# A mixture-of-experts kernel: 102 of 105 expert blocks in the main loop, the last three behind a branch at the end

## The chip, the core and the metric

The kernel runs on one core of a Trainium2 chip. A core has five engines with instruction queues of their own: TensorE (PE, matrix products; its weight loads are listed as PEld), VectorE (DVE), ScalarE (ACT), GpSimd (POOL) and SyncE (SP, which here only issues transfers), and 16 DMA engines that move data between DRAM and the on-chip memory. The engines run side by side and wait for each other by semaphores. The metric is the device time of one execution in microseconds (us).

## What is computed

The input `x` has the shape (2, 256, 56, 56): two images of N = 3136 positions and C = 256 channels. The first layer is a linear attention without softmax, with batch norm, residual and ReLU. The second layer treats the positions as tokens: layer norm, causal softmax attention with four heads, residual, and then a mixture of eight experts of which each token takes two. Only the last part matters here:

```python
probs = jax.nn.softmax(xf @ gate_w + gate_b, axis=-1)
top2_vals, top2_idx = jax.lax.top_k(probs, 2)
cw = jnp.zeros((N, Ee)).at[jnp.arange(N)[:, None], top2_idx].add(top2_vals)
# for each expert, added up with weight cw:
h = jax.nn.gelu(xf @ w1 + bb1, approximate=False)   # 256 -> 512
y = h @ w2 + bb2                                    # 512 -> 256
```

Here `xf` are all 6272 tokens of both images after a second layer norm. The result is added to the tokens before that norm and laid out as (2, 256, 56, 56) again. All arithmetic is in 32-bit floats.

## The kernel before, in words

A token and one of its two experts are a *pair*; there are 2 x 6272 = 12544 pairs, 98 blocks of 128. The experts' work is done block by block: 128 pairs of one expert at a time, so each expert rounds its pairs up to whole blocks. How many blocks are used depends on the data; it is at most `NBLK = (2*B*N + E*(P-1)) // P = 105`. The kernel of before always works on all 105; blocks that hold no pair are computed on rows of zeros and their results are dropped.

The order of the blocks serves the two images. Blocks 0 to 41 (`FULL0` = 42) hold pairs of image 0 alone; blocks 42 to 56 (`MIXED` = 57) hold the rest of image 0's full blocks, eight mixed ones and, where there is room, pairs of image 1; the remaining ones hold pairs of image 1, ordered by the token chunk at which they begin. That order is worked out on the chip, in `last_blocks` (L1180 and on): `upto` holds for each expert the running number of its last block, `eblks` the expert of each block, `qblk` its place in the table `x_slots`, `b1bs` its first bias. Blocks without pairs come last.

`experts` (L1296 to 1473) runs over the blocks with everything written out by hand, in an order that the kernel fixes (`manual_schedule`). In round `n` it fetches a group of `GB` = 3 blocks of rows six blocks ahead (`fetch`, on SP), prepares their target rows (`load`, three small DVE instructions), does the first product and the gelu of block `n` (`hidden`: 8 matrix products into `ht` in two passes each, L1398, and four gelus on ACT, L1407), transposes the rows of block `n + 2` (`inputs`, `tp`, L1375), copies the first weights of a later block next to the products (`weights`, 0.7 us on DVE, L1386), and does the second product of block `n - 3` (`outputs`, `LATE` = 3: `yp`, L1417). `outputs` adds the second bias on DVE into `ys` (L1427) and writes it out. Blocks below 57 go to `y_slots` by SP, blocks from 42 on go to `y_tokens` by an indirect transfer on POOL (a scatter, L1434), one row per pair; a row that holds no pair gets an address out of bounds and is not written. `worked[0]` counts the blocks whose outputs have been issued.

At the end of each round `between()` pulls two or three steps of side work from a queue of generators. The side work in this stage is `finish(0)` and `finish(1)`, which build the output of the two images in pieces of two token chunks (12 pieces of 256 tokens, numbered 0, 2, ... 22 by their first chunk, and piece 24 of 64). For image 1 a piece is loaded from `y_tokens` (two transfers on SP, L1516, one for each of the two experts' results), added to the residual `t` with the gate's weights (`add`, DVE, L1529), transposed (`store`, TensorE into `yo`, L1541), copied (ACT, L1546) and stored (SP, L1547). A piece may be loaded when all blocks that can hold its tokens are done: `complete(n)` is the number of blocks that this takes, 57 + 2n for a piece that ends before chunk n, and at most 105. `GAP` = 2 rounds are waited beyond that, and again between load and add. When the blocks are through (`over`), the rest of the pieces is drained as fast as it goes. A load waits on SP for the scatters of the blocks that it needs, and SP works in order.

At the very end each engine reads the small integer `good` and compares it with 128: a number that `judge` (L1588) computed from the softmax sums. If the sums were out of range, a second, general version of the layer runs; on these inputs it doesn't, and each engine jumps over it.

Of the kernel before, what the change touches and what calls it, by code (L numbers as in the profile page):

```python
# [9 lines left out]
F32 = mybir.dt.float32  # L10
U32 = mybir.dt.uint32
I32 = mybir.dt.int32
AF = mybir.ActivationFunctionType
ALU = mybir.AluOpType
AX = mybir.AxisListType
PSUM = bass.MemoryType.PSUM
# [3 lines left out]
SP = mybir.EngineType.SP  # L20
# [7 lines left out]
def conv_attn_moe_kernel(  # L28
# [47 lines left out]

    nc = tc.nc
    P = 128  # L80
    B, C, N = x.shape
    NH = C // P
# [4 lines left out]
    E = gate_w.shape[1]  # L87
    H = w1.shape[2]
    KH = H // P
    NCH = -(-N // P)  # L90
# [7 lines left out]
    XS = C + 2  # L98

    OFF = 16 * N  # L100
    FULL0 = -(-(2 * N - E * (P - 1)) // P)
    MOST0 = 2 * N // P
    MIXED = MOST0 + E
    NBLK = (2 * B * N + E * (P - 1)) // P
    GB = 3
    SCALE = 1.0 / HS**0.5
    LEAST, MOST = 1e-25, 1e25
    assert B == 2 and NBLK % GB == 0 and FULL0 % GB == 0 and QB % (2 * P) == 0
# [5 lines left out]
    def pairs(first=0, end=NCH):  # L114

        n = first
        while n < end:
            m = 2 if n + 1 < end and chunk(n + 1) == P else 1
            yield n, m, chunk(n)
            n += m  # L120

    const = ctx.enter_context(tc.tile_pool(name="const", bufs=1))
    tok = ctx.enter_context(tc.tile_pool(name="tok", bufs=1))

    ident = const.tile([P, P], F32, name="ident")
# [9 lines left out]
    def rows(name):  # L135
        t = room(name)[:, : NCH * XW].rearrange("p (n w) -> p n w", w=XW)
        if chunk(NCH - 1) < P:
            nc.gpsimd.memset(t[chunk(NCH - 1) :, NCH - 1, :], 0.0)
        return t
# [15 lines left out]
    def stats(b, n, m, k, pool, nm):  # L155

        for a in range(m):
            st6 = pool.tile([P, 6], F32, tag="st6", name=f"st6_{nm}_{n}_{a}")
            nc.vector.bn_stats(st6[:k], ts[b][:k, n + a, :C])
            nc.vector.bn_aggr(ts[b][:k, n + a, MEAN : MEAN + 2], st6[:k])  # L160

    def inverse_deviation(b, n, m):
        r = ts[b][:, n : n + m, RSTD]

        d = ts[b][:, n : n + m, SLOT]
        nc.scalar.activation(d, r, AF.Sqrt, bias=eps5)
        nc.vector.reciprocal(r, d)
# [258 lines left out]
    early = const.tile([P, MIXED], F32, name="early")  # L426
    wts = [const.tile([P, NCH, 2], F32, name=f"wt{b}") for b in range(B)]
    sums = const.tile([P, NSUM, 2 * W // P], F32, name="sums")
    good = const.tile([1, 1], I32, name="good")

    def empty_slots(b):
        nc.sync.dma_start(
# [6 lines left out]
    def layer1(nm, general):  # L439

        with ExitStack() as whole:
# [7 lines left out]
            def bank(name, shape=(P, 512)):  # L449
                return pm.tile(list(shape), F32, tag="m", name=f"{name}_{nm}")  # L450
# [484 lines left out]
            def dispatch(b):  # L935
# [244 lines left out]
                def last_blocks():  # L1180
# [5 lines left out]
                    def col(name, w=1):  # L1186
                        return g1.tile([R, w], F32, tag=name, name=f"{name}_{nm}")
# [3 lines left out]
                    edge = few("edge")  # L1191
                    nc.vector.tensor_scalar(edge[:, :1], nfull, float(E), None, ALU.add)
                    nc.vector.tensor_tensor(upto, upto, edge[:, :1].to_broadcast([P, E]), ALU.add)
                    past = col("c_past", E)
                    nc.vector.tensor_tensor(past, upto[:R], num.to_broadcast([R, E]), ALU.is_le)
                    hot = col("c_hot", E)
# [99 lines left out]
            def experts(w1s, w2s, b2s, ex, es, ps6, between, need, written):  # L1296
# [153 lines left out]
                        written()  # L1450

                fetched, groups, ids, xin, wb, act = [], [], [], {}, {}, {}
                for n in range(-1, NBLK + LATE):
                    while len(fetched) * GB <= min(n + 6, NBLK - 1):
                        fetched.append(fetch(len(fetched)))
                    while len(groups) * GB <= min(n + 3, NBLK - 1):
                        groups.append(load(len(groups), *fetched[len(groups)]))
                    if n < 0:
                        ids.extend(experts_of(0))
                    if 0 <= n < NBLK:  # L1460
                        act[n] = hidden(n, xin.pop(n), wb.pop(n))
                    for m in (n + 1, n + 2):
                        if m < NBLK and m > n + 1 - (n < 0):
                            xin[m] = inputs(m, groups[m // GB])
                    for m in (n + 1, n + 2):
                        if m < NBLK and m not in wb:
                            wb[m] = weights(m)
                    if 0 <= n - LATE < NBLK:
                        outputs(n - LATE, act.pop(n - LATE))

                    if len(ids) <= min(n + 3, NBLK - 1):
                        ids.extend(experts_of(len(ids) // GB))
                    between()

            def finish(b, oy, bufs):
# [27 lines left out]
                def complete(n):  # L1503


                    return min(NBLK, (2 * N + 2 * n * P) // P + E)

                def load(n, m, k):

# [14 lines left out]
                    return n, m, k, ys, t[:k, n : n + m, :C]  # L1524

                def add(n, m, k, ys, rows):
                    for a in range(m):
                        for c, y in enumerate(ys):
                            nc.vector.scalar_tensor_tensor(  # L1529
                                rows[:, a], y[:k, a], wts[b][:k, n + a, c : c + 1],  # L1530
                                rows[:, a], ALU.mult, ALU.add,
                            )
                        yield True

                def store(n, m, k, ys, rows):
                    w = (m - 1) * P + k
                    ot = oy.tile([P, NH, 2 * P], F32, tag="ot", bufs=2, name=f"ot_{nm}{b}_{n}")
                    yo = bank(f"yo_{b}_{n}", (P, NH, 2 * P))
                    for o in range(NH):
                        for a in range(m):  # L1540
                            nc.tensor.transpose(  # L1541
                                yo[:, o, a * P : a * P + k],
                                rows[:, a, o * P : (o + 1) * P],
                                ident[:k, :k],
                            )
                    nc.scalar.copy(ot[:, :, :w], yo[:, :, :w])  # L1546
                    nc.sync.dma_start(  # L1547
                        out=out[b, :, n * P : n * P + w].rearrange("(c p) n -> p c n", p=P),
                        in_=ot[:, :, :w],
                    )  # L1550
# [17 lines left out]
                GAP = 2  # L1568
                while parts or ahead or added:
                    now = worked[0]  # L1570
                    over = now == NBLK
                    if parts and len(ahead) < bufs:
                        n, m, k = parts[0]
                        if over or now >= complete(n + m) + GAP:
                            ahead.append((now, load(*parts.popleft())))
                            yield True
                            continue
                    if added and (over or now > added[0]):
                        store(*added[1])
                        added = None  # L1580
                        yield True
                    elif ahead and not added and (over or now >= ahead[0][0] + GAP):
                        yield from add(*ahead[0][1])
                        added = now, ahead.popleft()[1]
                    else:
                        yield False

            def judge():  # L1588

                tiles = g1.tile([P, 4], F32, tag="judge", name=f"judge_{nm}")  # L1590
                flat_sums = sums.rearrange("p r f -> p (r f)")
                nc.vector.tensor_reduce(tiles[:, 0:1], flat_sums, AX.X, ALU.max)
                nc.vector.tensor_reduce(tiles[:, 1:2], flat_sums, AX.X, ALU.min)
                yield True
                nc.vector.tensor_scalar(tiles[:, 2:3], tiles[:, 0:1], MOST, None, ALU.is_le)
                nc.vector.tensor_scalar(tiles[:, 3:4], tiles[:, 1:2], LEAST, None, ALU.is_ge)
                nc.vector.tensor_tensor(tiles[:, 2:3], tiles[:, 2:3], tiles[:, 3:4], ALU.mult)
                yield True
                yield True
                gdp = bank("gdp")  # L1600
                nc.tensor.matmul(gdp[:1, :1], tiles[:, 2:3], ones[:, 0:1], start=True, stop=True)
                nc.vector.tensor_copy(good, gdp[:1, :1])


            queue = deque()
# [167 lines left out]
            with ExitStack() as moe:  # L1773
# [40 lines left out]
                while queue:  # L1814
                    pull()

    layer1("f", False)

    n_good = nc.values_load(
        good, min_val=0, max_val=P,  # L1820
        skip_runtime_bounds_check_because="a count of at most P rows",
    )
    with tc.If(n_good < P):
        ts[0] = rows("t0g")
        for b in range(B):
            nc.sync.dma_start(out=ts[b][:, :, :C], in_=kept[b])
            with tc.tile_pool(name=f"r{b}", bufs=2) as rs:
                for n, m, k in pairs():
                    stats(b, n, m, k, rs, f"r{b}")
            inverse_deviation(b, 0, NCH)  # L1830
        layer1("g", True)


# [50 lines left out]
```

## Time and profile before

| | |
|---|---|
| time, median of 10 runs | 1319.36 us (1317.81 to 1321.12) |
| the profiled execution | 1318.74 us |
| its span, first to last instruction | 1317.0 us |
| mean TensorE clock granted | 0.993 |
| TensorE busy, 0 to 150 us (first layer) | 140.3 us |
| TensorE busy, 150 to 860 us (attention) | 700.9 us |
| TensorE busy, 860 to 1299.5 us (experts, with what is left of the attention) | 433.5 us |
| TensorE busy, 1299.5 to 1317 us (drain and end) | 2.3 us |
| `ht` matrix passes (L1398) | 1680, first at 881.9, last at 1290.7 us |
| scatters to `y_tokens` (L1434) | 63, last at 1299.3 us |
| loads from `y_tokens` (L1516) | 26, last at 1303.8 us |

A product in 32-bit floats shows as two or more passes, so a block has 16 passes of `ht`. In lists of instructions "x16" is the number of them, a name such as `ht_f<-xT_f,w_f` is the tile written and the tiles read, and "L1398" the line. In the chain of work that ended last, each row is a start, a length and the work, and each piece of work was what the next one waited for.

### The profile page before, as it was taken

To read this page: it belongs to the slowest core of one execution; us is meant where nothing else is said; L and a number is where in the kernel's file an instruction comes from. 1 tells how busy PE (TensorE), PEld (TensorE's weight loads), DVE (VectorE), ACT (ScalarE), POOL (GpSimd) and SP (SyncE) were. 2 spreads that over 40 slices of the span, in tenths; PEclk is the share of its full clock that TensorE was granted. 3 is DMA by queue.
4 is the path that set the end of the run, shared out by engine and by line. 5 is a ranking of instruction groups with operands and counts; after the bars stand their busy time and mean duration, and the time that the engine had idled before them with its cause. 6 is when DMAs were issued, how large, how long until landed. Compare 5 with 4: busy or idle time off the path is not lost.

```text
span 1317.0 us, 28242 instructions
## 1 busy us (share of the span) xinstructions
PE 1277.1 (97%) x10647; PEld 813.6 (62%) x10647; DVE 793.2 (60%) x1693; ACT 606.9 (46%) x1241; POOL 311.8 (24%) x300
## 2 busy tenths in 40 slices
PE   8999999999999999999999999999999999999995
PEld 7875444444444444444344444448999999999994
DVE  1582556657777754666868787864765443556552
ACT  0145554555555555455554456562433333344441
POOL 1113110100000111110003572000067112765541
PEclk9999999999999999999999999999999999999997
DMA  9993000000000000100001225241245333666552
GB/s 305 384 327 128 16 24 25 24 16 25 9 17 10 19 6 9 34 16 15 9 9 40 69 83 167 76 141 41 73 149 170 114 113 97 187 212 193 187 154 72
DMA packets 111048, 123.96 MB, mean 94 GB/s; under 512 B 20095, under 2 KB 100620, under 8 KB 110904
## 3 DMA queue, kind: packets, MB, share of 16 engines
q1 hardware_dynamic: 96664, 92.89, 22.6%
q0 software_dynamic: 10416, 26.00, 5.9%
q10 hardware_dynamic: 3824, 3.18, 0.8%
q8 instruction: 88, 1.44, 0.5%
q14 instruction: 56, 0.46, 0.1%
HBM read 63.04 MB, written 60.81 MB: 94 GB/s over the span
## 4 chain that ended last, share of the span: by engine, by line
PE 90%; DVE 3%; DMA 2%; ACT 1%; issue 1%; POOL 0%; SPq 0%; DVEq 0%; POOLq 0%; ACTq 0%
PE yp_f L689 20%; PE sc_f L649 19%; PE ht_f L1398 14%; PE yp_f L1417 13%; PE qk_f L535 7%; PE v_f L554 4%; PE pp_f L598 4%; PE cp L321 3%; PE gram L252 3%; PE tp_f L1375 2%; DVE acc_f L671 1%; PE sp_f L716 1%; ACT st_f L657 1%; PE yo_f L1541 1%; PE xp_f L514 1%
## 5 line engine op out<-in xcount | busy, mean ns | idle before, releaser
L657 ACT ACTIVATE st_f<-sc_f 128x896 f32<-128x896 f32 (+5 forms) x400 | 333.7, 837 | 294.4 <-PE sc_f L649 265.4
L671 DVE TENSOR_TENSOR acc_f<-acc_f,st_f 128x896 f32<-128x896 f32 (+5 forms) x372 | 366.4, 985 | 161.0 <-ACT st_f L657 153.4
L689 PE MATMUL yp_f<-st_f,v_f 64*64 64x448 f32 (+6 forms) x3184 | 340.4, 503 | 10.0 <-DVE qT_f L700 8.2
L649 PE MATMUL sc_f<-qT_f,kT_f 64*64 64x448 f32 (+6 forms) x3184 | 341.3, 500 | 0.0
L1407 ACT ACTIVATE g_f<-ht_f,b1b 128x128 f32<-128x128 f32 x420 | 119.8, 368 | 224.9 <-PE ht_f L1398 224.8
L689 PEld LDWEIGHTS yp_f<-st_f,v_f 64*64 64x64 f32 x3184 | 112.2, 133 | 162.9 <-issue 131.6
L649 PEld LDWEIGHTS sc_f<-qT_f,kT_f 64*64 64x64 f32 x3184 | 117.0, 133 | 151.3 <-issue 137.0
L1398 PE MATMUL ht_f<-xT_f,w_f 128*128 128x128 f32 x1680 | 206.6, 276 | 2.7 <-DVE w_f L1386 2.7
L1398 PEld LDWEIGHTS ht_f<-xT_f,w_f 128*128 128x128 f32 x1680 | 202.9, 193 | 7.9 <-issue 3.3
L497 POOL TENSOR_SCALAR xn_f<-t 128x256 f32<-128x256 f32 (+1 forms) x50 | 68.2, 1371 | 541.7 <-issue 331.1
L1279 POOL DMA_INDIRECT x_slots<-xr_f,idx x100 | 113.4, 1134 | 203.6 <-DVE xr_f L1271 111.6
L1386 DVE COPY w_f<-w1s_f 128x1024 f32 x105 | 73.3, 699 | 60.5 <-PE ht_f L1398 60.2
L1434 POOL DMA_INDIRECT y_tokens<-ys_f,to_f x63 | 64.5, 1024 | 135.8 <-DVE ys_f L1427 109.2
L1427 DVE TENSOR_TENSOR ys_f<-yp_f,kT_f 128x128 f32<-128x128 f32 x105 | 30.5, 291 | 105.9 <-PE yp_f L1417 105.2
L535 PE MATMUL qk_f<-px_f,wat 128*128 128x512 f32 (+1 forms) x224 | 92.6, 558 | 1.2 <-ACT px_f L520 1.2
L659 DVE TENSOR_TENSOR st_f<-st_f,keep 128x256 f32<-128x256 f32 (+1 forms) x112 | 44.1, 394 | 68.2 <-ACT st_f L657 67.8
L535 PEld LDWEIGHTS qk_f<-px_f,wat 128*128 128x128 f32 x224 | 38.7, 190 | 54.3 <-issue 44.6
L1417 PE MATMUL yp_f<-px_f,g_f 128*128 x210 | 63.0, 382 | 0.0
L1417 PE MATMUL yp_f<-kT_f,g_f 128*128 x210 | 62.5, 379 | 0.0
L1417 PE MATMUL yp_f<-w2s_f,g_f 128*128 x210 | 62.5, 379 | 0.0
L1417 PE MATMUL yp_f<-v_f,g_f 128*128 x210 | 62.5, 379 | 0.0
L1491 POOL DMA_INDIRECT y_f<-y_slots,idx x50 | 55.9, 1118 | 16.3 <-issue 13.7
(256 smaller groups left out, 1172.0 us busy)
## 6 DMA issues: line engine op xcount, KB each, us to landing
x_slots<-fill SPq DMA_DIRECT2D x1, 8127.0 KB
xb_f<-x_slots SPq DMA_DIRECT2D x63, 129.0 KB
x_slots<-fill SPq DMA_DIRECT2D x1, 7296.0 KB
y_slots<-ys_f SPq DMA_DIRECT2D x57, 128.0 KB
kept<-t SPq DMA_DIRECT2D x2, 3200.0 KB
x<-in_x_dram SPq DMA_DIRECT2D x14, 448.0 KB
xr<-in_x_rows_dram SPq DMA_DIRECT2D x12, 512.0 KB
out_dram<-ot_f SPq DMA_DIRECT2D x24, 256.0 KB
```

What stands on the lines that cost most here:

```text
L497: nc.gpsimd.tensor_scalar(xn[:k, a], ts[b][:k, n + a, :C], ts[b][:k, n + a, MEAN : MEAN + 1], ts[b][:k, n + a, RSTD : RSTD + 1], ALU.subtr ...
L535: nc.tensor.matmul(ps[:, :w], wat[:, c, d0 : d0 + P], xT[:, c, :w], start=(c == 0), stop=(c == NH - 1),)
L649: nc.tensor.matmul(ps[h : h + HS, a, c0:W], kT[hp][rows, j * P + h : j * P + h + HS], qT[rows, hp, q0 + c0 : q0 + W], start=True, stop=True,)
L657: nc.scalar.activation(st[:k, :, c0:], ps[:k, :, c0:W], AF.Exp, scale=SCALE)
L671: nc.vector.tensor_tensor(acc[:k, :, c0:], acc[:k, :, c0:], st[:k, :, c0:], ALU.add)
L689: nc.tensor.matmul(yp[a * HS : (a + 1) * HS, h // HS, c0:W], v[hp][h : h + HS, j, a, :HS], st[h : h + HS, a, c0:], start=first, stop=bool( ...
L1279: s = nc.gpsimd.indirect_dma_start(out=xds[b], out_offset=bass.IndirectOffsetOnAxis(ap=idxs[b][:kk, k, n : n + 1], axis=0), in_=xr[:kk], i ...
L1386: nc.vector.tensor_copy(w, w1s[:, :, bass.ds(e, 1), :].rearrange("p c e h -> p c (e h)"))
L1398: nc.tensor.matmul(ht[:, k, :], w[:, c, k * P : (k + 1) * P], xT[:, c, :], start=(c == 0), stop=(c == NH - 1),)
L1407: nc.scalar.activation(g[:, k, :], ht[:, k, :], AF.Gelu, bias=b1bs[b][:, k, i : i + 1])
L1417: nc.tensor.matmul(yp[:, :C], g[:, k, :], w2s[k][:, bass.ds(e, 1), :].rearrange("p e d -> p (e d)"), start=(k == 0), stop=(k == KH - 1),)
L1434: s = nc.gpsimd.indirect_dma_start(out=y_tokens, out_offset=bass.IndirectOffsetOnAxis(ap=to[:, n % GB : n % GB + 1], axis=0), in_=ys, in_o ...
```

## The change

The main loop runs over `MAIN = NBLK - GB` = 102 blocks. A flag `fits` says whether the blocks used are at most 102; it is multiplied into a second integer next to `good`. At the end the engines read the second integer first. Where it is below 128 (the sums were out of range, or more than 102 blocks are used) they go into a branch; in it the first integer is read and the general version run where that is needed, and then `late()` works on the last three blocks, loads all pieces of image 1 again and stores them again.

For that the residual `t` must outlive the main loop: the adds of image 1 now write into the loaded tile `y0` and no longer into `t`, the transposes read `y0`, and a piece that is added but not yet transposed counts against the three buffers. The condition for loading a piece is changed near the end, `complete` is cut at 102, and `judge` waits until the order of image 1's blocks is known.

```diff
+    MAIN = NBLK - GB
...
-    good = const.tile([1, 1], I32, name="good")
+    good = const.tile([1, 2], I32, name="good")
+    fits = const.tile([P, 1], F32, name="fits")
...
+                    nc.vector.tensor_scalar(fits, upto[:, E - 1 :], float(MAIN), None, ALU.is_le)
...
-                for n in range(-1, NBLK + LATE):
+                for n in range(-1, MAIN + LATE):
...
-                    return min(NBLK, (2 * N + 2 * n * P) // P + E)
+                    return min(MAIN, (2 * N + 2 * n * P) // P + E)
...
                 def add(n, m, k, ys, rows):
+                    to = ys[0][:k] if b else rows
                     for a in range(m):
                         for c, y in enumerate(ys):
                             nc.vector.scalar_tensor_tensor(
-                                rows[:, a], y[:k, a], wts[b][:k, n + a, c : c + 1],
-                                rows[:, a], ALU.mult, ALU.add,
+                                to[:, a], y[:k, a], wts[b][:k, n + a, c : c + 1],
+                                to[:, a] if c else rows[:, a], ALU.mult, ALU.add,
                             )
...
                 def store(n, m, k, ys, rows):
+                    rows = ys[0][:k] if b else rows
...
-                    over = now == NBLK
-                    if parts and len(ahead) < bufs:
+                    over = now == MAIN
+                    if parts and len(ahead) + bool(added) < bufs:
                         n, m, k = parts[0]
-                        if over or now >= complete(n + m) + GAP:
+                        of = complete(n + m)
+                        if over or now >= min(of + GAP, max(of, MAIN - 1)):
...
             def judge():
+                while not ranked[B - 1]:
+                    yield False
...
-                nc.vector.tensor_copy(good, gdp[:1, :1])
+                nc.vector.tensor_copy(good[:, 0:1], gdp[:1, :1])
+                nc.vector.tensor_tensor(good[:, 1:2], gdp[:1, :1], fits[:1], ALU.mult)
...
+    def late():
+        b = B - 1
+        table = xds[b].rearrange("(n p) w -> n p w", p=P)
...
+            for n in range(MAIN, NBLK):
...
+                w1e = lt.tile([P, NH, H], F32, tag="w1", name=f"w1_{n}")
+                nc.sync.dma_start(
+                    out=w1e, in_=w1[bass.ds(e, 1)].rearrange("o (c p) h -> p (o c) h", p=P)
+                )
...
+            for n, m, k in pairs():
+                w = (m - 1) * P + k
+                both = [lt.tile([P, 2, C], F32, tag=f"y{c}", name=f"y{c}_{n}") for c in range(2)]
...
-    n_good = nc.values_load(
-        good, min_val=0, max_val=P,
-        skip_runtime_bounds_check_because="a count of at most P rows",
-    )
-    with tc.If(n_good < P):
...
+    n_done = count(1)
+    with tc.If(n_done < P):
+        n_good = count(0)
+        with tc.If(n_good < P):
...
+            layer1("g", True)
+        late()
```

In `late()` each tile has one buffer; a block loads its weights (0.5 MB each for `w1` and `w2`), bias and rows, does both products and scatters its results, and each piece of image 1 is then loaded, added, transposed, copied and stored as in `finish(1)`. All other uses of `NBLK` in `experts` become `MAIN`. Tables and constants keep the size for 105 blocks.

## The prediction

> **What bounds the kernel now.** I read the page's head first, then the tail of the chain that ended last, then the timeline of the last 50 us and the DMA traffic by windows. The page's head, and the shares of the chain by engine:
>
> ```profile
> span 1317.0 us, 28242 instructions
> PE 1277.1 (97%) x10647; PEld 813.6 (62%) x10647; DVE 793.2 (60%) x1693; ACT 606.9 (46%) x1241; POOL 311.8 (24%) x300
> ...
> PE 90%; DVE 3%; DMA 2%; ACT 1%; issue 1%; POOL 0%; SPq 0%; DVEq 0%; POOLq 0%; ACTq 0%
> ```
>
> TensorE is busy for 97% of the span and carries 90% of the chain: TensorE work that goes away in the middle of this program comes off the end. The chain near the end (start us, length, what):
>
> ```profile
> 1278.20 1.79 PE ht_f L1398 x16
> 1281.93 1.78 PE ht_f L1398 x16
> 1285.66 1.78 PE ht_f L1398 x16
> 1289.18 1.78 PE ht_f L1398 x16
> ```
>
> These are the hidden layers of blocks 101, 102, 103 and 104. One block follows another every 3.73 us: 1.78 for the 16 passes of `ht`, 1.73 for 8 pairs of `yp`, 0.2 for two transposes of a later block. The last step is 3.52, since no later block is left to transpose. After block 104 comes the drain: the outputs of four blocks, then the pieces of `finish(1)` that were waiting for them. The chain there:
>
> ```profile
> 1298.57 0.48 DVE ys_f L1427 x2
> 1299.05 0.28 DVE t L1529
> 1299.32 2.67 DMA y_tokens<-ys_f,to_f
> ...
> 1302.13 2.87 DMA y_f<-y_tokens
> 1305.00 0.03 issue
> 1305.03 1.38 DVE t L1529 x3
> ```
>
> The last block's `ys` goes to DRAM by a scatter (2.67), the last four gathers wait for it on SP (2.87), then come adds, transposes, copy and store. From `ys` at 1298.57 to the end of the span it is 18.4 us in which TensorE does almost nothing. That part is hung onto the last block, wherever that block ends.
>
> Last, whether blocks 102 to 104 hold pairs. The scatters of blocks 99 to 104 start on POOL at 1286.47, 1289.98 (100), 1293.49 (101), 1295.66, 1297.39 and 1299.32. A scatter writes only rows that hold a pair. The software queue's packets, MB and share in the windows 1286 to 1290, 1290 to 1293.5, 1295.6 to 1297.3, 1297.3 to 1299.3 and 1299.3 to 1302.5:
>
> ```profile
> q0 software_dynamic: 48, 0.09, 7.1%
> q0 software_dynamic: 48, 0.05, 4.0%
> q0 software_dynamic: 41, 0.00, 1.5%
> q0 software_dynamic: 96, 0.00, 3.1%
> q0 software_dynamic: 48, 0.00, 1.0%
> ```
>
> Every scatter has 48 packets, but from block 101 on they move under 0.005 MB, four rows of 1 KB at most. The reference's routing gives the rest: on the given inputs the eight experts get 2348, 1997, 1599, 1862, 967, 862, 1283 and 1626 pairs, in blocks of 128 that is 19+16+13+15+8+7+11+13 = 102. Block 101 holds the three pairs by which 1283 exceeds ten blocks, 102 to 104 hold none. `upto[E-1]` is then 102, `fits` is 1 with nothing to spare, and the branch is not taken. To reach 103 an expert would need 34 more pairs, which rounding doesn't give.
>
> **The change part by part.** I write T for the start of the last hidden layer; before, T = 1289.02 (block 104, timeline).
>
> 1. *Three blocks fewer.* 48 passes of `ht`, 24 pairs of `yp`, 6 transposes, three 0.69 us weight copies on DVE, 12 gelus, three fetches, three scatters. On the path only TensorE's share counts: 3 x 3.73 = **-11.19 us**. The same result from the other side: block 101's hidden layer starts at 1278.04 and loses the 0.21 of the transposes ahead of it, so T becomes 1277.83. The DVE, ACT and POOL work lay beside TensorE and is worth nothing by itself.
>
> 2. *A different drain order.* In the program as built, `finish(1)` now adds piece 18 on DVE between `ys` of block 100 and `ys` of block 101, and transposes it behind the last `yp`. Before, that add lay beside block 104's hidden layer, and its four transposes (1292.53 to 1292.96, 0.43) sat between two `yp`. From the rows: `ys` of block 103 began at 1296.62 = T + 7.60; without the 0.43 the corresponding one (block 100) begins at T + 7.17 and ends by T + 7.67. The add of piece 18 takes 4 x 0.48 = 1.92, to T + 9.59, and the last `ys` begins there; TensorE would have been ready at T + 8.9. Before, the last `ys` began at 1298.57 = T + 9.55, itself held by a half add of piece 20 that waited for its load. Net **0 to +0.1**. If the add were out of the way, -0.65.
>
> 3. *Piece 20 moves behind the last block's outputs.* Its loads wait on SP for the scatter of block 100: POOL at T + 7.17 + 0.77 = T + 7.94, plus 2.81 (from 1299.32 to 1302.13), issued at T + 10.75, landed 2.9 later at T + 13.65; its four adds end at T + 15.6. Piece 22's loads wait for the last scatter: T + 9.59 + 0.75 + 2.81 = T + 13.15 (before T + 13.11), landed at T + 16.0. The adds of piece 20 fit into that wait: **0**. If the cover were gone, if its loads landed together with those of 22, they would cost 1.92.
>
> 4. *Loads ahead limited to three buffers counting the added one* (the add now writes into `y0` instead of `t`). The loads of 16, 18 and 20 are issued at 1263.31, 1279.44 and 1294.42, 15 us apart, so the limit binds only at the end: piece 24's loads stand on SP behind the store of piece 18. That store costs 0.38 on SP before its 256 KB move; a like store filled 16 DMA engines for 0.9 us (1294.6 to 1295.6). The order before had 24's loads directly behind 22's. DVE took 22's four adds until 1306.70 and then 24's, so there was a little slack: **0 to +0.9**, I take +0.2, nearer to the SP row, since the transfer overlaps the adds of 22. The store of piece 20 (issued about T + 16.9) also runs ahead of 22's (T + 19.4) with 2.5 us between: 0.
>
> 5. *Small instructions.* `fits` and `good[1]` are two DVE instructions, beside the `good` cast of 0.135 us at 1026.1, where DVE is busy 235 of 440 us in the expert stage: 0. `judge` stays where it was, as its new condition is already true there. Adds and transposes keep their shapes (0.484 and 0.27 us).
>
> 6. *The jump at the end.* One read of `good` and one compare per engine on the skipped path, as before. SP's read starts at 1309.4 and the span ends 7.6 us later. Bounds: 0 (the same path), and up to 7 for a second such jump, which the built program doesn't have on this path; I take 0.
>
> The Trainium skill, "Runtime: NRT & Kernel Launch", section "Instruction fetch mechanics", says that a taken branch out of the current pages stalls for a fetch by DMA. It speaks against nested branches; by it a second taken jump would leave about -4 instead of -11. In the window from 1307 on the instruction queues move 8 packets, which agrees that there is a fetch, and there it already is before.
>
> Sum: -11.19 + 0.05 + 0 + 0.2 + 0 + 0 = **-10.9**. The profiled execution took 1318.74 (span 1317.0, 1.74 around it), so it would become 1307.8, with a span of about 1306.1. The median of the ten runs, 1319.36, lies 0.6 above the profiled one: **1308.4 us** for the median.
>
> **The rivals.**
>
> *A: the drain gives part back* (15%). Items 3 and 4 both go to their upper ends: +1.92 for the adds of piece 20, +0.9 for the store in front of 24's loads. For it: the drain holds three pieces where it held two and a half. Against: 2.4 us of waiting on DVE in which 20 has room. 1308.4 + 2.6 = 1311.0.
>
> *B: more than three bare blocks goes* (14%). In the stretch 1230 to 1278, block pitches of 4.17 and 4.6 stand beside those of 3.73, because transposes of the finish pieces are put between. If the piece moved into the drain is hidden (item 2 at its lower end, -0.65, and item 4 at 0), the time is 1308.4 - 0.9 = 1307.5; with a full 4.0 per block, 1306.6. Against: that work is only moved, not removed.
>
> *C: the branch is taken* (2%), the one that ends slower. From 103 used blocks on, `late()` runs with single buffers: 13 pieces, each a load (2.87), adds (1.9), transposes, copy and store (about 1.2, 0.6 and 2.7) one after the other, about 9 x 13 = 120 us, and three blocks, each with 1 MB of weights (0.26 MB took 0.9, so 3.6), a block (3.7) and a scatter (2.7), 10 each: about 150, or 1458 us. Against it stand the empty scatters and the 102 above.
>
> *D: the end of the program costs more* (3%). A second jump of the length in item 6, +7: 1315.4. Against: only one is on the path.
>
> **How the numbers follow.** Forecast 66%, A 15%, B 14%, D 3%, C 2%. The range takes in A and B and the 1.6 us by which single runs of the same kernel stray from their median: 1305.8 to 1311.6. 0.2% is 2.6 us, about what a measurement of this kernel can tell from no change. All cases but C, and a sliver of D, are faster by more than that: 0.97 faster, 0.01 same, 0.02 slower.
>
> **What would show it.** In the changed profile: `ht` 1632 times instead of 1680, `yp` groups of 204 instead of 210, 60 scatters instead of 63; the last `ht` group of the chain near 1278.0; last scatter near 1288.2; three loads of pieces 20, 22, 24 behind it with 22's at about 1291.0; no instruction of `late`; span 1306. If the last scatter is at 1288 but the span ends after 1307.5, items 3, 4 or 6 were wrong; if instructions of `late` appear, the count of blocks was. If the pitch of the blocks in mid-stage is not 3.73 to 4.2 any more, something changed outside these steps.

## The result and the profile after

The changed kernel takes 1307.59 us (median of 8 runs, 1307.17 to 1309.98) against 1318.69 us for the kernel before (28 runs). The ratio is 0.9917, with a 95% interval of 0.9908 to 0.9926: 11 us faster. The forecast was 1308.4 us, in a range of 1305.8 to 1311.6, and 97% for faster.

The profiled execution took 1307.41 us, with a span of 1305.7. The head of its page, and its groups of `ht`, of the scatters and of the second bias:

```profile
span 1305.7 us, 28014 instructions
PE 1266.4 (97%) x10569; PEld 802.3 (61%) x10569; DVE 789.5 (60%) x1683; ACT 602.8 (46%) x1226; POOL 309.2 (24%) x297
...
L1403 PE MATMUL ht_f<-xT_f,w_f 128*128 128x128 f32 x1632 | 199.6, 275 | 2.9 <-DVE w_f L1391 2.9
...
L1439 POOL DMA_INDIRECT y_tokens<-ys_f,to_f x60 | 61.2, 1020 | 127.4 <-DVE ys_f L1432 102.9
L1432 DVE TENSOR_TENSOR ys_f<-yp_f,kT_f 128x128 f32<-128x128 f32 x102 | 29.7, 291 | 102.0 <-PE yp_f L1422 101.7
```

There are 1632 passes, 60 scatters and 102 blocks, and no line of `late()` appears: the branch was not taken. TensorE is busy for 10.7 us less. The end of the chain, from block 100 on (start us, length, what):

```profile
1273.69 1.98 PE ht_f L1403 x16
1277.84 1.79 PE ht_f L1403 x16
1279.63 5.20 PE yp_f L1422 x24
1287.84 3.59 DMA y_tokens<-ys_f,to_f
1291.56 2.69 DMA y_f<-y_tokens
```

The last hidden layer in the chain stands at 1277.84, where the prediction had it near 1278.0; before, it was at 1289.18. That is 11.34 us. From there to the end of the span it is 27.86 us against 27.82. So the whole gain lies ahead of the drain. The timeline shows where. The passes of block 57, the first one behind the mixed blocks, and of the last block, before and then after:

```profile
1104.17 1.95 PE L1398 MATMUL ht_f<-xT_f,w_f 128*128 128x128 f32 x16
1289.02 1.95 PE L1398 MATMUL ht_f<-xT_f,w_f 128*128 128x128 f32 x16
...
1104.03 1.95 PE L1403 MATMUL ht_f<-xT_f,w_f 128*128 128x128 f32 x16
1277.68 1.95 PE L1403 MATMUL ht_f<-xT_f,w_f 128*128 128x128 f32 x16
```

From block 57 to the last block it is 184.85 us before and 173.65 after, 11.20 less. Each step from block to block between them is the same in both traces to 0.02 us, but for the last one, into block 101, which lacks the transposes of a later block (4.05 us against 4.27). The other 0.14 lies ahead of block 57.

The drain itself didn't stay the same, though: two changes in it cancel. SP's read of `good` in the two profiles, by tile, with its duration in ns and the time of its first and last start:

```profile
L1819 SPq TENSOR_LOAD <-good x1: 555/555/555, 1309.4 to 1309.4; - x1
L1931 SPq TENSOR_LOAD <-good x1: 562/562/562, 1298.7 to 1298.7; - x1
```

The traces give these distances, in us from the start T of the last hidden layer's passes (1289.02 before, 1277.68 after):

| | before | after |
|---|---|---|
| last scatter starts | 10.31 | 10.16 |
| first load of piece 22 issued | 13.12 | 13.88 |
| adds of piece 22 begin | 16.01 | 16.59 |
| SP reads `good` | 20.37 | 21.00 |
| from SP's read to the end of the span | 7.63 | 7.01 |

The drain lost 0.63 us up to SP's read. The stretch between the scatter and the load that waits for it lost 0.91, and an earlier scatter (0.15) and shorter loads (0.18) gave part of that back. The stretch after SP's read, the closing code, won 0.62. The experiments below look at both.

### The profile page after: what moved, and what is told of

Its sections match the earlier page's. It is cut to its first block, busy times and chain, and to the rows that moved or that the text cites. A ratio compares the mean times of both kernels' runs of the same rounds, so it can differ in the third digit from the quotient of the medians.

```text
span 1305.7 us, 28014 instructions
## 1 busy us (share of the span) xinstructions
PE 1266.4 (97%) x10569; PEld 802.3 (61%) x10569; DVE 789.5 (60%) x1683; ACT 602.8 (46%) x1226; POOL 309.2 (24%) x297
## 4 chain that ended last, share of the span: by engine, by line
PE 90%; DVE 3%; DMA 2%; issue 1%; ACT 1%; POOL 0%; SPq 0%; POOLq 0%; DVEq 0%; ACTq 0%
PE yp_f L693 20%; PE sc_f L653 19%; PE ht_f L1403 14%; PE yp_f L1422 13%; PE qk_f L539 7%; PE v_f L558 4%; PE pp_f L602 3%; PE cp L324 3%; PE gram L255 3%; PE tp_f L1380 2%; DVE acc_f L675 1%; PE sp_f L720 1%; PE yo_f L1549 1%; ACT st_f L661 1%; PE xp_f L518 1%
## 5 line engine op out<-in xcount | busy, mean ns | idle before, releaser
L1412 ACT ACTIVATE g_f<-ht_f,b1b 128x128 f32<-128x128 f32 x408 | 116.3, 368 | 217.1 <-PE ht_f L1403 217.1
L1403 PE MATMUL ht_f<-xT_f,w_f 128*128 128x128 f32 x1632 | 199.6, 275 | 2.9 <-DVE w_f L1391 2.9
L1403 PEld LDWEIGHTS ht_f<-xT_f,w_f 128*128 128x128 f32 x1632 | 195.9, 192 | 8.2 <-issue 3.8
L1439 POOL DMA_INDIRECT y_tokens<-ys_f,to_f x60 | 61.2, 1020 | 127.4 <-DVE ys_f L1432 102.9
```

What stands on the lines that cost most here:

```text
L1403: nc.tensor.matmul(ht[:, k, :], w[:, c, k * P : (k + 1) * P], xT[:, c, :], start=(c == 0), stop=(c == NH - 1),)
L1412: nc.scalar.activation(g[:, k, :], ht[:, k, :], AF.Gelu, bias=b1bs[b][:, k, i : i + 1])
L1439: s = nc.gpsimd.indirect_dma_start(out=y_tokens, out_offset=bass.IndirectOffsetOnAxis(ap=to[:, n % GB : n % GB + 1], axis=0), in_=ys, in_o ...
```

## The experiments

The kernels of one group ran on the same chip beside the kernel before. In the third group every kernel, the one before included, took about 30 us longer, so that times are compared within a group and the drain by its distances from T. These are, for all profiles (us; "landing" is from the last scatter's start to the first load that waits for it, "closing" from SP's read to the end of the span):

| profile | landing | adds of 22 begin | SP reads `good` | closing | T to end |
|---|---|---|---|---|---|
| before | 2.81 | 16.01 | 20.37 | 7.63 | 28.00 |
| changed | 3.72 | 16.59 | 21.00 | 7.01 | 28.01 |
| changed, again | 3.71 | 16.64 | 21.32 | 7.02 | 28.34 |
| changed, third | 3.49 | 16.88 | 21.21 | 6.97 | 28.18 |
| all 105 blocks | 2.84 | 16.16 | 21.00 | 5.90 | 26.90 |
| no late branch | 3.85 | 17.17 | 21.43 | 5.60 | 27.02 |
| old loading rule | 3.59 | 16.68 | 21.15 | 6.93 | 28.08 |
| add behind | 2.91 | 15.63 | 20.07 | 7.00 | 27.07 |
| four buffers | 4.13 | 17.05 | 21.35 | 6.91 | 28.26 |
| longer body | 3.37 | 16.64 | 20.91 | 5.84 | 26.76 |
| add behind, longer body | 2.89 | 15.55 | 20.06 | 5.74 | 25.80 |
| the same, again | 2.89 | 16.02 | 20.46 | 5.72 | 26.18 |
| piece 20 held | 2.67 | 19.10 | 23.36 | 7.06 | 30.42 |

T itself strays by about a microsecond between executions of one program (1277.68 and 1278.65 for the changed kernel on like chips), which is most of the scatter of the times. The straying comes ahead of block 57: from there to the last block both take 173.65 us.

### The change without the removal

```diff
-    MAIN = NBLK - GB
+    MAIN = NBLK
```

> All of the change is kept, but the main loop runs over all 105 blocks (the branch at the end has no blocks left to work on). My theory: the whole gain of 11.1 us is the three blocks (3 x 3.73 = 11.19), and the other edits come to nothing: about 1318.8 us, within 0.6 of the kernel before, a span of about 1317. Rival: the new drain order or the smaller instructions give or cost something of their own; then it lies 1 us or more off the kernel before, on either side, and a pitch other than 3.73 per block pays for the rest.

Measured: 1317.75 us against 1319.07, ratio 0.9989 (0.9980 to 0.9998). Almost the whole gain goes with the three blocks, but not all: 1.3 us remain, which by the expectation's numbers is the rival. The table tells where most of it is, and it isn't the drain order. From T to SP's read this kernel takes 0.63 us longer than the kernel before, and from there to the end it is 1.73 us shorter. (In this profile T is 1290.69, 1.7 later than before, which is straying: from block 57 to the last block it takes the same 184.85 us.) SP's read of `good` in its profile; the span was 1317.6:

```profile
L1931 SPq TENSOR_LOAD <-good x1: 562/562/562, 1311.7 to 1311.7; - x1
```

From 1311.7 to 1317.6 it is 5.9 us, where the kernel before takes 7.6. SP runs down the same closing instructions in both.

### Without the late branch

```diff
-    n_done = count(1)
-    with tc.If(n_done < P):
-        n_good = count(0)
-        with tc.If(n_good < P):
...
-        late()
+    n_good = count(0)
+    with tc.If(n_good < P):
...
```

> The main loop has 102 blocks as in the change, but the branch at the end is the one of before: the second integer isn't read and the late blocks aren't in the program (so that on inputs with more than 102 used blocks results would be missing; on these there are none). My theory: the skipped path has one read and one jump either way, so 1307.6 us, within 0.5 of the changed kernel. Rival: the longer body to jump over or the second condition costs time; then it is faster than the changed kernel by 1 us or more, and the 7.0 us from SP's read of good to the end of the span shrink.

Measured: 1307.10 us, ratio 0.9909 (0.9894 to 0.9924); the interval can't tell it from the changed kernel. The profile can: up to SP's read nothing is gained, and the closing stretch shrinks from 7.0 to 5.6, the sign that the rival named. But a longer jump can't be the reason alone: the kernel before, which has the same single condition and no `late()`, has the longest closing stretch of all (further down it is shown why).

### The branch taken

```diff
-  nc.vector.tensor_scalar(fits, upto[:, E - 1 :], float(MAIN), None, ALU.is_le)
+  nc.vector.tensor_scalar(fits, upto[:, E - 1 :], float(MAIN - 1), None, ALU.is_le)
```

> The flag is compared with 101 in place of 102 blocks, so that the branch is taken on these inputs and the last three blocks (empty) and all 13 pieces of image 1 are worked on after the main loop. This prices the rival in which the branch is taken: the prediction's working gives 13 x 9.3 + 3 x 10 = 150 us, so about 1458 us. If the pieces overlap across engines even with single buffers, it is less (about 13 x 6 + 20 = 98, 1406 us); if each wait is longer than in the drain, more.

Measured: 1429.8 us (one run), a span of 1428.1, so the branch costs 122 us where the prediction had 150. The chain inside it, from the last of the three late blocks' scatters (L1905 to L1918 are the loads, adds and transposes of the pieces):

```profile
1347.52 2.07 DMA y_tokens<-ys,to
...
1349.74 2.84 DMA y<-y_tokens
...
1353.93 1.13 PE yo L1918 x4
1355.08 3.35 DMA y<-y_tokens
...
1361.05 2.88 DMA y<-y_tokens
...
1366.55 3.24 DMA y<-y_tokens
```

A piece takes 5.3 to 6.3 us, not 9.3: the next one is loaded as soon as the transposes have freed the buffers, while copy and store of the last one still run. The three blocks take 46 us together (1303.9 to 1349.7), 15 each instead of 10. The rival's direction stands, and its price was 28 us too high; its weight hung on the count of blocks alone, and that was right.

### The changed kernel again, and three changes in the drain

> The changed kernel once more, as the measure for the three beside it: 1307.6 us, span about 1305.7, the last scatter landing 3.6 us after its start and 22's adds 16.6 us after the start of the last hidden layer.

Measured: 1308.71 us against 1319.74, ratio 0.9915 (0.9899 to 0.9930).

The first of the three beside it undoes the loading rule near the end:

```diff
-                        if over or now >= min(of + GAP, max(of, MAIN - 1)):
+                        if over or now >= of + GAP:
```

> Only the new loading rule near the end is undone: a piece is loaded two rounds after its blocks are complete or when the blocks are through, as before, so piece 20's loads move from behind the scatter of block 100 to behind that of block 101. My theory: the cover of item 3 is gone, 20's loads (0.5 MB) and adds (1.75 to 1.92 us) come onto the path ahead of piece 22: 1.5 to 2.5 us slower than the changed kernel, about 1309.5 us; and the last scatter lands in about 2.7 us instead of 3.6, since 20's loads no longer move at the same time, which gives 0.9 of it back. Rival: the drain is set by the last scatter and its piece alone: within 0.3 of the changed kernel.

Measured: 1308.10 us, ratio 0.9912 (0.9896 to 0.9928), the same as the changed kernel in every column of the table. The expectation was wrong because the edit does nothing: piece 20's loads are pulled a step later, but nothing is issued on SP in between, and they wait for the scatter of block 100 either way. SP's instructions and TensorE's products stand in the same order in both kernels. So the new loading rule has no part in the result, and this run is one more repetition.

The second takes the add of piece 18 out of the way of the last `ys`:

```diff
-                    elif ahead and not added and (over or now >= ahead[0][0] + GAP):
+                    elif ahead and not added and (over or ahead[0][0] + GAP <= now < MAIN - 1):
```

> The add of piece 18 is no longer issued ahead of the last block's ys on DVE; it comes behind it, when the blocks are through. My theory: the last ys starts 0.5 us earlier (TensorE is ready for it at 8.9 us after the start of the last hidden layer, it starts at 9.4), and with it the last scatter and the loads of piece 22: 0.3 to 0.5 us faster than the changed kernel, about 1307.2 us. Rival: the scatter lands no earlier, because it shares the DMA engines with piece 20's loads that were issued just before, and the adds of 18 and 20 then both lie ahead of 22's on DVE: no change, or up to 1 us slower.

Measured: 1306.93 us, ratio 0.9900 (0.9883 to 0.9917), an interval that overlaps with that of the changed kernel beside it; the profile tells more. The chain of the drain in its profile, whose T is 1278.11:

```profile
1287.77 2.78 DMA y_tokens<-ys_f,to_f
...
1290.68 3.04 DMA y_f<-y_tokens
1293.74 0.73 DVE y_f L1536 x2
```

The last scatter starts 0.50 us earlier (T + 9.66), as expected, and then it also lands faster, in 2.78 us instead of 3.59. Piece 22's adds begin 1.0 us earlier and SP's read comes 0.9 to 1.3 us earlier, about twice what the theory gave. The rival had the right part in mind, transfers that share the DMA engines, with the wrong sign. SP's loads of pieces 20 and 22 (the first of four starts the row) in the changed kernel and here:

```profile
1287.98 4.45 SPq L1521 DMA_DIRECT2D y_f<-y_tokens  x4
1288.41 3.14 SPq L1521 DMA_DIRECT2D y_f<-y_tokens  x4
```

In the changed kernel the scatter starts at T + 10.16 and piece 20's loads are issued at T + 10.31, almost together. Here the scatter has 0.64 us of lead.

The third gives image 1's pieces a fourth buffer:

```diff
-                queue.appendleft(finish(1, oy, 3))
+                queue.appendleft(finish(1, oy, 4))
```

> Image 1's pieces get four buffers in place of three, so that piece 24's loads are issued directly behind 22's and ahead of the store of piece 18. My theory (item 4): the store in front costs little, since 24's adds come behind 22's on DVE anyhow: 0 to 0.4 us faster than the changed kernel. Rival: the store's 256 KB delay the last piece by their whole 0.9 us: 0.7 us or more faster.

Measured: 1307.65 us, ratio 0.9911 (0.9896 to 0.9926), and T to the end 28.26 us: no gain. Piece 24's adds began at T + 18.63, in the changed kernel at T + 18.67 and 18.65. The store in front of its loads costs nothing, since the adds of 22 are what they follow.

### The landing of the last scatter, and the closing code

> The changed kernel a third time, as the measure for the three beside it: a median between 1307.4 and 1308.8 us; from the last hidden layer in the chain to SP's read of good about 21 us, and 7.0 us from there to the end of the span, with a pause of 1.2 to 1.3 us in SP's closing waits.

Measured: 1337.11 us against 1349.82, ratio 0.9909 (0.9887 to 0.9930). The ratio is the same as on the other chips. The landing was 3.5 and the closing 6.97.

In the next kernel the loads of piece 20 wait for the last scatter too:

```diff
-                        if over or now >= min(of + GAP, max(of, MAIN - 1)):
+                        if over or now >= of + GAP:
...
-                            if block >= complete(n + m):
+                            if block >= complete(n + m) and worked[0] < MAIN:
```

> Piece 20's loads are made to wait for the scatter of block 101 as well, what the earlier run with the old loading rule should have done and didn't, since there the loads stood at the same place on SP and waited for the same scatter of block 100. My theory: the last scatter no longer shares the DMA engines with 20's 0.5 MB and lands in 2.7 to 2.8 us instead of 3.5 to 3.6, but 20's loads and adds are then on the path (0.9 of issuing and 1.75 of adds ahead of 22's adds): 22's adds begin 17.3 us after the last hidden layer instead of 16.4, about 0.9 us slower than the changed kernel. Rival: the slow landing is the scatter's own and stays at 3.5: then 1.7 us slower. Other rival: the drain hides it all: within 0.3.

Measured: 1339.71 us, ratio 0.9926 (0.9909 to 0.9943); T to the end 30.42 us in its one profile, 2.2 more than the changed kernel beside it (by time the intervals overlap). The drain of its profile, T = 1306.42:

```profile
1316.58 2.48 DMA y_tokens<-ys_f,to_f
...
1320.24 5.25 DMA y_f<-y_tokens
1325.52 0.74 DVE y_f L1536 x2
```

The scatter, now alone, lands in 2.48 us: the slow landing is not its own, it comes with piece 20's 0.5 MB. The price of holding them was sized too low, 0.9: the loads of 22 now stand behind 20's and take 5.25 us instead of 2.7 to 3.2, so 22's adds begin 2.2 us later. So piece 20's loads are better left where they are: their traffic costs the scatter 0.8 us here, and holding them back costs more than it saves.

The last two look at the closing code. In the traces each engine, after its jump over the branch, pauses before the first instruction of its closing code, and then runs down a row of waits. In some builds one engine pauses a second time in the middle of that row (us):

```
kernel           engine  jump at   first wait after  second pause   end of span
before           POOL    1299.67   2.67              2.02           1317.02
before           SP      1310.01   2.87              none           1317.02
changed          SP      1299.30   2.70              1.25           1305.69
all 105 blocks   SP      1312.31   2.91              none           1317.59
no late branch   SP      1300.49   2.63              none           1305.47
```

In the kernel before, POOL's pause of 2.0 us comes ahead of its closing wait, the longest of the three `DRAIN` instructions in this row:

```profile
L1880 POOLq DRAIN  x3: 40/107/8981, 1307.2 to 1316.7; - x3
```

It takes 9.0 us from its start there (8.7 or 9.0 in the other builds). POOL then ends at 1316.18, 1.75 us after SP has closed. That is why that kernel has the longest closing stretch. In the changed kernel POOL has no such pause, but SP has one of 1.25, with four waits ahead of it and eight behind it:

```profile
L1997 SPq EVENT_SEMAPHORE  x4: 28/28/28, 1302.8 to 1303.0; - x4
L1997 SPq EVENT_SEMAPHORE  x8: 28/28/28, 1304.3 to 1304.7; - x8
```

The variants with another drain order have it too, 1.1 to 1.3 us long. In the profile of the changed kernel a packet of instructions moves in that pause; the DMA traffic from 1303 to 1304.3 us holds nothing else:

```profile
DMA packets 1, 0.02 MB, mean 13 GB/s; under 512 B 0, under 2 KB 0, under 8 KB 0
## 3 DMA queue, kind: packets, MB, share of 16 engines
q8 instruction: 1, 0.02, 4.2%
```

The packet is a hint and no more. In the second profile of the changed kernel SP pauses from 1304.44 to 1305.57, and no packet starts in that time; the last one of 16 KB starts at 1303.38, ahead of it. And the kernel with the longer body, below, has such a packet at 1332.27 and no pause. Still, the closing code may lie across a border of what is fetched at once. The next kernel moves it without running anything more:

```diff
+            spare = lt.tile([P, 8], F32, name="spare")
+            for _ in range(20):
+                nc.sync.dma_start(out=spare, in_=table[0][:, :8])
             for n in range(MAIN, NBLK):
```

> 20 further small transfers on SP stand in the branch that isn't taken, so nothing more is executed; only the code behind the branch lies 20 to 60 instructions further on in SP's stream. My theory: SP's closing code lies across the border of two blocks of code that are fetched apart (a pause of 1.2 to 1.3 us in its closing waits in every profile of this build, an 8 KB instruction fetch beside it, and none in the builds with 105 blocks or without the late blocks), and moving it puts it into one block: SP's read to the end of the span 5.7 to 6.0 us instead of 7.0, 1.0 to 1.3 us faster than the changed kernel. Rival: the pause belongs to something else at the end (the last store's landing, a wait for another engine): it stays, 7.0 us.

Measured: 1335.72 us against 1337.11 for the changed kernel beside it, ratio 0.9892 (0.9875 to 0.9909), too near to tell by time. In the profile the closing stretch is 5.84 us, where every profile without the 20 transfers but with the late branch and 102 blocks has 6.91 to 7.06, and SP's second pause is gone. SP's read and the span of this profile are 1328.2 and 1334.0:

```profile
L1934 SPq TENSOR_LOAD <-good x1: 557/557/557, 1328.2 to 1328.2; - x1
```

A longer body to jump over makes the end shorter. The rival, a wait for a transfer or another engine, is out: the waits are the same, and in the changed kernel the semaphores of the wait behind the pause were last updated at 1302.2, before the pause began.

Both edits that shorten the end, together:

> Both edits that shorten the end: the add of piece 18 behind the last ys, and the 20 transfers in the branch not taken. My theory: the two are independent, 1.0 us before SP's read of good (20.0 instead of 21.0 from the last hidden layer) and 1.2 behind it: about 1305.6 us, 2.2 us faster than the changed kernel beside it. Rival: behind SP's read another engine then ends last (POOL's closing wait takes 8.7 us from its start in every profile) and only part of the second gain shows: 1306.3.

Measured: 1336.83 us, ratio 0.9906 (0.9890 to 0.9921). By time that shows nothing, on a chip on which single runs of one kernel lay almost 9 us apart; by the profile, T to the end is 25.80 us, 2.4 less than beside it, about what the two gave one by one (0.9 to 1.3 and 1.4). Once more on another chip:

> Both edits that shorten the end once more, since the chip of the run before was some 30 us slower from its start and strayed more. My theory: from the last hidden layer to the end of the span 25.8 us as in that profile, against 28.0 to 28.3 in the three profiles of the changed kernel, so a ratio to the kernel before of about 0.990 (1305.6 to 1318.7 us), where the changed kernel had 0.9909 to 0.9917. Rival: what the end gains is lost ahead of it, and the ratio stays at 0.9915.

Measured: 1305.43 us (1304.42 to 1306.24, 4 runs) against 1319.31, ratio 0.9898 (0.9881 to 0.9914). The drain in its profile, whose span is 1302.7 and T 1276.51:

```profile
1286.17 2.76 DMA y_tokens<-ys_f,to_f
...
1289.07 3.44 DMA y_f<-y_tokens
1292.53 0.80 DVE y_f L1536 x2
```

T to the end is 26.18 us. All four runs lie below all eight of the changed kernel, but they weren't timed side by side with these, and the intervals of the two ratios overlap (0.9908 to 0.9926 for the changed kernel). By the distance from T to the end it is the shortest version here; by ratio it can't be told from either edit alone (0.9900 and 0.9892).

## Why the prediction was right, point by point

- *What bounds the kernel.* TensorE in the block stage, and a drain hung onto the last block: shown. T moved by 11.34 us, T to the end by 0.01; that this second number is so small is luck (items 3 and 6).
- *The branch is not taken.* Right: 102 used blocks, no line of `late()`. The kernel with the flag one lower shows that it would have cost 122 us; the prediction's rival C had 150.
- *Item 1, -11.19.* From block 57 to the last block it is 11.20 us less, and with all 105 blocks it is the old 184.85 again, so this is shown nearly to the hundredth. (T itself moved by 11.34, with 0.14 from ahead of block 57, where it strays.) The times agree: by the ratios the kernel with all 105 blocks lies 9.5 us behind the changed kernel, with about 1.7 to either side, and the changed kernel pays 1.1 of closing that the other doesn't.
- *Item 2, 0 to +0.1.* The last scatter started at T + 10.16 (T + 10.34 by the sum), so the item came out at -0.15. The add of piece 18 in the way was real and worth 0.5, not 0.65, by the kernel that moves it.
- *Item 3, 0.* Its timing was right within half a microsecond for piece 20 itself: loads at T + 10.31 and adds at T + 13.58, 10.75 and 13.65 by the sum. Wrong was the landing of the last scatter, taken as 2.81 to the next load from the row of before. It was 3.72, because piece 20's loads move at the same time. Two runs show this cause: 2.9 with a lead of 0.64 us, 2.67 with the loads held. This is a term of +0.9 that the sum lacked.
- *Item 4, +0.2.* The store in front of piece 24's loads cost nothing (four buffers).
- *Item 5, 0.* Nothing in the runs speaks against it; it was not tested by itself.
- *Item 6, 0.* The stretch behind SP's read lost 0.62 us. The prediction took one jump for as good as another, and it followed SP's path to the end, where in the kernel before POOL's closed last, 1.75 us behind SP's. The closing stretches of 5.6 to 7.6 us differ by an engine's second pause. For SP, where its closing code lies decides on that pause, shown by the longer body; for POOL's pause in the kernel before no run tests it.

The sum of -10.9 came out at -11.1 in the medians. That it is so near owes something to luck in two misses: +0.63 in the drain against +0.25 forecast for items 2 to 4, and -0.62 in the closing against 0.

Rival A, the drain that gives part back, had the place right, with a smaller size (0.63 instead of 2.6), but neither of its two terms was the cause: 20's adds were hidden and the store cost nothing; it was the landing of the scatter. Rival B had no part: the steps between blocks are the same, and piece 18 in the drain was not hidden. Of rival D's seven microseconds nothing came; the stretch became shorter.

## What to carry to other kernels

Work that no data needs can be taken out of a bound engine's loop at its full price, if a count says from the data when it is needed and the repair stands behind a branch. The price is read from the pitch of the blocks in the chain, and what hangs on the last block moves along. In a drain look at what is issued in the same half microsecond as the transfer on the path: a large load started about 0.15 us after a scatter cost it 0.5 to 1.2 us here (a landing of 3.4 to 3.9 us against 2.7 to 2.9), and 0.6 us of lead avoided that. Of two builds that differ by a microsecond or two, compare the closing stretch before explaining the rest by the edit.

## What was not expected of the hardware

- The same closing code took from 5.6 to 7.6 us from SP's read to the end of the span, constant within 0.1 us for each build over its profiles (7.01, 7.02, 6.97 for the changed kernel) and moved by 1.2 us by 20 transfers in code that never runs. The Trainium skill, "Runtime: NRT & Kernel Launch", section "Instruction fetch mechanics", says that instructions are fetched in blocks and that a taken branch out of the blocks at hand stalls for a fetch; the first pause of 2.6 to 2.9 us on SP agrees with it. That the second pause is the fetch of the next block is inferred from its going away when the code is moved, and not shown: the packets of instructions don't line up with it in every profile, and which packet belongs to which engine the trace doesn't tell.
- A scatter that writes no rows is not free: those of the empty blocks before had 48 packets like any other, and the last one, without data, landed in 2.67 us.
